# Toeplitz coefficients in pieces among projections, and zero rows written behind the input statistics

## The chip, the cores and the metric

One core of a Trainium2 chip runs one launch of the whole network. The metric is the device time of that launch in microseconds; the median of three runs of the kernel before is 5857.68 us. TensorE (PE) multiplies matrices into PSUM, VectorE (DVE) and ScalarE (ACT) read PSUM and SBUF, GpSimd (POOL) works on SBUF, and SyncE (SP) issues most DMA transfers; POOL issues some. Each engine takes its instructions in a fixed order.

## The reference

Four layers follow each other on x of shape (8, 56, 56, 192), each as `x = x + layer(groupnorm(x))`. Layers 0 and 1 are a gated Toeplitz block, layer 2 a depthwise convolution with an MLP, layer 3 window attention. The change concerns the first block (576 = D1 hidden channels):

```python
p, q, v = silu(x @ p_w.T + p_b), silu(x @ q_w.T + q_b), silu(x @ v_w.T + v_b)
gamma = (0.95 + 0.05 * clip(slope, 0, 1)) ** arange(1, n)
a1 = rpe_mlp(rpe_input, t1...) * decay     # 2n coefficients for each channel
a2 = rpe_mlp(rpe_input, t2...) * decay
qv = q * v
o1 = toeplitz(qv along the width, a1)
o2 = toeplitz(qv along the height, a2)
out = (p * (o1 + o2)) @ o_w.T + o_b
```

The coefficients `a1` and `a2` depend on weights alone: a small MLP of 32 units with three hidden layers, evaluated at 111 distances, times powers of a decay. The group norm in front of the block needs the mean and variance of each sample pair's whole input.

## The kernel before

Samples lie in four pairs j = 0 to 3, channels on partitions, tokens along the free axis (T = 3136). The first stage of `tno_layers` goes as follows.

`input_stats` loads the input of a pair in seven tiles `x` of 448 tokens (pool `tab`, seven buffers, line 213), VectorE takes their statistics (line 215), and `pair_gn_finish` turns them into scale and shift `gn` (lines 71 to 97).

`tno_qv` makes q*v for two pairs. Tiles `t6` of 256 tokens are loaded, normalized by ScalarE (line 243) and multiplied by the weights `wq` on TensorE in units of 128 tokens by up to 512 output columns (`unit`, line 260). Each tile of 128 tokens has two units of 512 columns and one of 128. VectorE moves a unit out of PSUM with the bias added (line 269, into one of three `t8` buffers), ScalarE takes SiLU (line 298), GpSimd multiplies q by v (line 301, into one of three `t4` buffers), and SyncE stores the product to `qv` in DRAM (line 304). The first four tiles of tokens are done as half units (lines 281 and 288, kept in buffers `z0` to `z11`), first for pair 0 and then for pair 1, since pair 1's statistics come later. All PSUM results rotate through four `bank2` tiles.

`decay_tables` makes the Toeplitz coefficients of one layer. VectorE makes powers of the decay into five `pw` tiles (lines 146 to 158). For each of the two directions it evaluates the MLP: line 175 the input layer, line 179 three matmuls with VectorE's ReLU (line 181) after each, line 185 five matmuls for the outputs. VectorE multiplies each output by the powers into a tile `a` (line 192, two buffers, cleared at the end by GpSimd, line 189), and SyncE writes it with a shift per row to the table in DRAM (line 202, 240 KB matrices are read from it later at line 389). The function is called once for each layer: 12 matmuls at line 179, 20 at line 185 and 72 table writes in both.

Two more writes fill what the Toeplitz stage reads beyond the data. A tile `none` of zeros is copied by a DMA of GpSimd's queue to the last eight rows of each image in both `qv` arrays (line 715, 4032 KB each), and four small ones to the last row of each table (line 719).

The order of this stage is not that of the source alone: the tile framework's scheduler orders it for each engine by dependences and its own estimates. From `in_order` on (the Toeplitz stage) TensorE, ScalarE, VectorE and GpSimd keep the order written. There `weave` runs the Toeplitz of one half beside the projections or outputs of another: it advances one generator as `lane` and calls the other, `steps`, for as much work as is due. A generator yields the time that its last piece is thought to take; `weave` spreads a total of `given` between the shares `lo` and `hi` of the lane.

The SP queue carries all loads, q*v stores and table writes in one order. In the kernel before, both zero writes stand at the head of GpSimd's queue, and each layer's 36 table writes stand in one block in SP's.

Of the kernel before, what the change touches and what calls it, by code (L numbers as in the profile page):

```python
# [12 lines left out]
F32 = mybir.dt.float32  # L13
# [16 lines left out]
TT = 448  # L30
NT = T // TT
D1 = 576
# [6 lines left out]
def view(ap, offset, dims):  # L39

    return bass.AP(ap.tensor, ap.offset + offset, [ap.ap[0], *dims])


class Net:
# [91 lines left out]
    def decay_tables(self, L, p, tables):  # L136

        nc, inp = self.nc, self.inp
        tv = p.tile([32, 111], F32, name="tv", bufs=1)
        nc.sync.dma_start(tv, inp["tvec"])  # L140
        pows = []
        for c in range(5):
            m = min(128, D1 - 128 * c)
            sl = p.tile([128, 1], F32, name="sl")
            nc.sync.dma_start(sl[:m], inp[f"{L}_slope"][128 * c : 128 * c + m, :])
            nc.vector.tensor_scalar(sl[:m], sl[:m], 0.0, 1.0, ALU.max, ALU.min)
            nc.vector.tensor_scalar(sl[:m], sl[:m], 1.0 - 0.95, 0.95, ALU.mult, ALU.add)
            pw = p.tile([128, 64], F32, name="pw", bufs=5)
            nc.gpsimd.memset(pw[:m, 0:1], 1.0)
            n = 1  # L150
            while n < 64:
                nc.vector.tensor_scalar(
                    pw[:m, n : 2 * n], pw[:m, 0:n], sl[:m], None, ALU.mult
                )
                n *= 2
                if n < 64:
                    sq = p.tile([128, 1], F32, name="sl")
                    nc.vector.tensor_mul(sq[:m], sl[:m], sl[:m])
                    sl = sq
            pows.append(pw)  # L160
        for d in range(2):
            t = f"{L}_t{d + 1}"
            w0 = p.tile([32, 2], F32, name="w0")
            nc.sync.dma_start(w0[:, 0:1], inp[f"{t}_w0"])
            nc.sync.dma_start(w0[:, 1:2], inp[f"{t}_b0"])
            ws = p.tile([32, 3, 32], F32, name="ws")
            nc.sync.dma_start(ws, inp[f"{t}_ws"])
            bs = p.tile([32, 3], F32, name="bs")
            nc.sync.dma_start(bs, inp[f"{t}_bs"])
            wo = p.tile([32, D1], F32, name="wo")  # L170
            nc.sync.dma_start(wo, inp[f"{t}_wo"])
            bo = p.tile([128, 5], F32, name="bo")
            nc.sync.dma_start(bo, inp[f"{t}_bo"])
            h = p.tile([32, 111], F32, name="h")
            nc.vector.tensor_scalar(h, tv, w0[:, 0:1], w0[:, 1:2], ALU.mult, ALU.add)
            nc.vector.tensor_scalar(h, h, 0.0, None, ALU.max)
            for i in range(3):
                hp = self.bank2()[:32, 0, :111]
                nc.tensor.matmul(hp, ws[:, i, :], h, start=True, stop=True)
                h = p.tile([32, 111], F32, name="h")  # L180
                nc.vector.tensor_scalar(h, hp, bs[:, i : i + 1], 0.0, ALU.add, ALU.max)
            for c in range(5):
                m = min(128, D1 - 128 * c)
                ap = self.bank2()[:, 0, :111]
                nc.tensor.matmul(
                    ap[:m], wo[:, 128 * c : 128 * c + m], h, start=True, stop=True
                )
                a = p.tile([128, 4 * self.TG + 56], F32, name="a")
                nc.gpsimd.memset(a[:m, 111:], 0.0)
                back = view(pows[c][:m], 55, [[-1, 55]])  # L190
                for lo, hi, dec in ((0, 55, back), (55, 111, pows[c][:m, 0:56])):
                    nc.vector.scalar_tensor_tensor(
                        view(a[:m], 110 - lo, [[-1, hi - lo]]),
                        ap[:m, lo:hi],
                        bo[:m, c : c + 1],
                        dec,
                        ALU.add,
                        ALU.mult,
                    )
                for n in range(m // 32):  # L200
                    to = tables[d][self.TG * (4 * c + n) : self.TG * (4 * c + n + 1)]
                    nc.sync.dma_start(
                        to.rearrange("g (c w) -> c g w", w=self.TW),
                        view(a[32 * n : 32 * n + 32], 0, [[4, self.TG], [1, self.TW]]),
                    )

    def input_stats(self, xs, gn, j, p):

# [457 lines left out]
    def tno_layers(self, x0, x1, x2, gn, last):  # L666


        tc, nc = self.tc, self.nc
        LS = ("L0", "L1")  # L670
        tables = [

            [
                self.dram.tile([D1 // 32 * self.TG + 1, 32 * self.TW], F32, name=f"{L}_tab{d}")
                for d in range(2)
            ]
            for L in LS
        ]
        qvs = {

            j0: self.dram.tile([D1 // 32, 64 * W, 128], F32, name=f"qv{j0}") for j0 in (0, 2)
        }
        o = [self.dram.tile([B // 2, 9, 128, T], F32, name=f"{L}_sum") for L in LS]
        x = (x0, x1, x2)
        with ExitStack() as ctx, ExitStack() as wqp:
            self.wqp = wqp.enter_context(tc.tile_pool(name="wqp", bufs=1, side="right"))
            self.tp = ctx.enter_context(tc.tile_pool(name="tp", bufs=3))
            Q = lambda i, j0, apart=None: self.tno_qv(LS[i], j0, x[i], gn[i], qvs[j0], apart)
            O = lambda i, j0, woven=True: self.tno_out(LS[i], j0, x[i], gn[i], o[i], x[i + 1], gn[i + 1], woven)
            TZ = lambda i, j0: self.tno_toeplitz(j0, tables[i], qvs[j0], o[i])  # L690
            QT, OT, TZT = 25 * 2.25 * 5.3, 28 * 10.7, 8 + 72 * 3.2

            with tc.tile_pool(name="tab", bufs=2) as tab:
                stats = [self.input_stats(x0, gn[0], j, tab) for j in range(4)]
                for more in stats[0]:
                    pass
                first = Q(0, 0, tab)
                next(first)

                for n in range(14):  # L700
                    next(first)
                    next(stats[1], None)
                for more in stats[1]:
                    pass
                for n in range(10):
                    next(first)
                self.decay_tables("L0", tab, tables[0])
                for st in stats[2:]:
                    for more in st:
                        next(first)  # L710
                none = tab.tile([112, 512], F32, name="none", bufs=1)
                nc.gpsimd.memset(none, 0.0)
                for qv in qvs.values():
                    to = qv[:, T:].rearrange("n (p k) e -> p n (k e)", p=112)
                    nc.gpsimd.dma_start(to, view(none, 0, [[0, D1 // 32], [1, 512]]))
                self.decay_tables("L1", tab, tables[1])
                for t in tables:
                    for d in range(2):
                        nc.gpsimd.dma_start(t[d][D1 // 32 * self.TG :, :512], none[:1])
                lanes = [[(first, QT - 104.0)], [(Q(0, 2), QT)], [(O(0, 0), OT), (Q(1, 0), QT)]]  # L720
                lanes += [[(O(0, 2), OT), (Q(1, 2), QT)], [(O(1, 0), OT)], [(O(1, 2, False), OT)]]
                self.weave(lanes[0], None, lanes[1][0][0])
            in_order = tc.manual_schedule(engines=ENGINES)
            with tc.tile_pool(name="tz", bufs=1) as self.tz, in_order:
                self.tms = []
                for i in range(2):
                    self.tms.append(self.tz.tile([128, 32 * self.TW], F32, name=f"tm{i}"))
                for n, tz in enumerate((TZ(0, 0), TZ(0, 2), TZ(1, 0), TZ(1, 2))):
                    self.weave(lanes[n + 1], tz, lanes[n + 2][0][0], TZT)
                    if n == 2:  # L730
                        wqp.close()
            self.weave(lanes[5], **last())
# [908 lines left out]
```

## Time and profile before

| what | us |
|---|---|
| median of 3 runs | 5857.68 (5851.6 to 5859.38) |
| profiled execution, its own time | 5859.99 |
| span of its trace | 5858.2 |
| mean granted TensorE clock | 0.954 |
| seventh x tile's statistics start | 41.49 |
| first projection matmul (L281) | 52.68 |
| first matmul of full units (L260) | 154.51 |
| first Toeplitz matmul (L402) | 507.65 |

Busy time over the span: PE 5356.5 us (91%), DVE 2365.6 us (40%), ACT 2269.0 us (39%), POOL 2206.4 us (38%). In the page's slices, a digit is the busy share of 146 us in tenths. A row of a window table gives start and end, length, busy time and count for each engine, then the granted TensorE clock, the mean busy share of the 16 DMA engines and their rate in GB/s. In a timeline row, the bracket holds the idle time before the instruction and what ended it. The count of TensorE rows is that of passes, two for each float32 matmul.

### The profile page before, as it was taken

The numbers are of one execution on the slowest core, as the hardware profiler recorded it, in microseconds if no ns is written. First come the engines' busy times: TensorE is split into PE (matmuls) and PEld (weight loads), VectorE is DVE, ScalarE is ACT, GpSimd is POOL, SyncE is SP. The second block draws the span as 40 slices with busy tenths as digits, with TensorE's granted clock in tenths as the row PEclk, the third lists the DMA queues.
The fourth block names the chain that finished last, engine by engine and source line by source line (L and its number), as shares of the span: only waits on it lengthen the run. The fifth ranks groups of instructions, "written<-read, shape, count | busy, mean of one in ns | idle before, by whom it ended". The sixth has DMA issues, their size and how long they took to land.

```text
span 5858.2 us, 144266 instructions
## 1 busy us (share of the span) xinstructions
PE 5356.5 (91%) x64672; PEld 3886.7 (66%) x64672; DVE 2365.6 (40%) x3770; ACT 2269.0 (39%) x2990; POOL 2206.4 (38%) x1527
## 2 busy tenths in 40 slices
PE   5799888899999999999888799989999999889887
PEld 2577666677777777777666578856665445667666
DVE  5444554233454233553343322331222322556655
ACT  2244454444454444554444322242323333333332
POOL 1244566466556564565666300000001001333332
PEclk8799999999999999999999899999999999999998
DMA  8547998898787887987999465644444222344442
GB/s 268 110 144 219 267 287 245 220 264 275 214 237 217 239 258 224 254 249 196 312 296 293 168 210 205 230 125 161 150 160 121 64 64 62 75 97 86 89 92 56
DMA packets 1029770, 1098.79 MB, mean 188 GB/s; under 512 B 232768, under 2 KB 966976, under 8 KB 1013728
## 3 DMA queue, kind: packets, MB, share of 16 engines
q1 hardware_dynamic: 993568, 888.57, 55.5%
q0 software_dynamic: 35584, 200.99, 8.9%
q8 instruction: 509, 8.34, 0.6%
q14 instruction: 109, 0.89, 0.0%
HBM read 725.48 MB, written 363.94 MB: 186 GB/s over the span
## 4 chain that ended last, share of the span: by engine, by line
PE 57%; POOL 6%; SPq 6%; DMA 5%; DVE 5%; issue 3%; ACT 2%; POOLq 0%; DVEq 0%; ACTq 0%
PE bank L260 9%; PE bank L950 6%; PE bank L811 5%; PE bank L527 4%; PE bank L1030 4%; PE bank L572 4%; PE bank L402 4%; SPq L389 3%; PE bank L1044 3%; POOL s L424 2%; PE bank L1224 2%; PE bank L536 2%; PE bank L575 2%; SPq L376 2%; PE bank L1171 2%
## 5 line engine op out<-in xcount | busy, mean ns | idle before, releaser
L260 PE MATMUL bank<-wq,t 128*128 128x256 f32 (+4 forms) x7680 | 1286.6, 375 | 66.8 <-DVE t L269 36.3
L260 PEld LDWEIGHTS bank<-wq,t 128*128 128x128 f32 (+2 forms) x7680 | 1006.5, 191 | 348.1 <-issue 110.5
L269 DVE TENSOR_TENSOR t<-bank,wq 128x1024 f32<-128x1024 f32 (+3 forms) x480 | 517.8, 1111 | 776.6 <-PE bank L260 575.1
L301 POOL TENSOR_TENSOR t<-t 128x1024 f32<-128x1024 f32 (+2 forms) x288 | 518.7, 1815 | 692.4 <-ACT t L298 371.5
L409 ACT COPY ot<-bank 128x896 f32<-128x896 f32 x576 | 493.2, 914 | 626.8 <-PE bank L402 351.3
L424 POOL TENSOR_TENSOR s<-s,ot 128x1568 f32<-128x1568 f32 x144 | 618.3, 4298 | 70.0 <-DVE ot L422 69.3
L402 PE MATMUL bank<-q,tm 56*32 56x224 f32 x18432 | 525.6, 365 | 81.6 <-DMA tm<-L_tab 26.8
L298 ACT ACTIVATE t<-t 128x2048 f32<-128x2048 f32 (+2 forms) x288 | 422.0, 1488 | 405.7 <-DVE t L269 396.1
L402 PEld LDWEIGHTS bank<-q,tm 56*32 56x32 f32 x18432 | 354.4, 109 | 221.6 <-issue 115.8
L553 POOL TENSOR_TENSOR t<-t,t 128x896 f32<-128x896 f32 x168 | 347.3, 2085 | 358.4 <-DMA t<-L_sum 163.9
L527 PE MATMUL bank<-t,wo 128*128 128x224 f32 x1792 | 398.0, 378 | 46.6 <-ACT t L506 22.1
L585 DVE SCALAR_TENSOR_TENSOR t<-bank,wo,t 128x448 f32<-128x448 f32 x112 | 76.4, 682 | 886.3 <-ACT t L581 474.7
L950 PE MATMUL bank<-z,w 128*128 128x448 f32 (+1 forms) x1344 | 413.7, 555 | 1.9 <-ACT h L959 1.7
L527 PEld LDWEIGHTS bank<-t,wo 128*128 128x128 f32 x1792 | 352.4, 203 | 83.8 <-issue 31.7
L546 ACT ACTIVATE t<-bank,wo 128x448 f32<-128x448 f32 x448 | 248.1, 635 | 407.2 <-PE bank L536 379.2
L572 PE MATMUL bank<-t,wo 128*128 128x224 f32 x1792 | 378.1, 365 | 0.0
L127 POOL DMA_DIRECT2D x<-x x64 | 36.6, 573 | 859.7 <-DVE x L981 829.6
L572 PEld LDWEIGHTS bank<-t,wo 128*128 128x128 f32 x1792 | 337.2, 194 | 33.8 <-issue 32.2
L811 PEld LDWEIGHTS bank<-xt,cm 113*112 113x112 f32 x3072 | 315.0, 180 | 43.7 <-issue 38.3
L420 DVE STREAM_TRANSPOSE s<-ot 128x1792 f32<-128x1792 f32 x144 | 292.5, 2033 | 124.3 <-DMA L_sum<-s 102.1
L811 PE MATMUL bank<-xt,cm 113*112 113x108 f32 (+2 forms) x3072 | 326.2, 266 | 6.4 <-issue 3.3
L950 PEld LDWEIGHTS bank<-z,w 128*128 128x128 f32 (+1 forms) x1344 | 182.2, 189 | 205.7 <-issue 197.4
(148 smaller groups left out, 6991.3 us busy)
## 6 DMA issues: line engine op xcount, KB each, us to landing
q<-qv SPq DMA_DIRECT2D x36, 3584.0 KB
q<-qv SPq DMA_DIRECT2D x72, 1568.0 KB
L_sum<-s POOLq DMA_DIRECT2D x288, 392.0 KB, 7.4
t<-L_sum SPq DMA_DIRECT2D x112, 1008.0 KB
qv<-t SPq DMA_DIRECT2D x192, 512.0 KB
cm<-in_L_cm SPq DMA_DIRECT2D x96, 896.0 KB
tm<-L_tab SPq DMA_DIRECT2D x288, 240.0 KB
x<-t POOLq DMA_DIRECT2D x112, 336.0 KB, 7.1
```

Source lines behind the costliest of these rows:

```text
L260: nc.tensor.matmul(pp[:m, b, 256 * j : 256 * j + k], x[rows, j, 2 if part else b, s : s + m], w[rows, part, c0 + c : c0 + c + k],  start=p ...
L269: nc.vector.tensor_add(z[:m, c : c + k, :], view(pp[:m], 0, [[1, k], [256, 4]]), view(bias[:m], c0 + c, [[1, k], [0, 4]]),)
L298: nc.scalar.activation(z[:m, :n, :], z[:m, :n, :], AF.Silu)
L301: nc.gpsimd.tensor_mul(prod[:m, :k], half[:, :, 0], half[:, :, 1])
L402: nc.tensor.matmul(pt[32 * j : 32 * j + 32, r, hf * 224 : (hf + 1) * 224], tm[rows, at : at + 32], q[rows, :, 4 * c : 4 * c + 4], start=Tr ...
L409: nc.scalar.copy(view(ot, 4 * (g % 4), [[16, 2], [32, 112], [1, 4]]), view(pt, 0, [[512, 2], [4, 112], [1, 4]]),)
L424: nc.gpsimd.tensor_add(to, to, view(of, 0, [[1, 28], [32, 56]]))
L527: mm(gs[c // 2][:, b, c % 2 * 256 : c % 2 * 256 + N], pw[:, 0, 128 * c : 128 * c + 128], xn[:, b], start=c % 2 == 0, stop=False,)
L553: gate.tensor_mul(to, to, pg)
L572: mm(P[:, b, :N], ow[:, c, 0:128], g[:, 4 * b + c], start=False, stop=c == 3 and b == 1)
L811: nc.tensor.matmul(pc[:, 128 * e + 4 * m0 : 128 * e + 4 * m1], cm[:113, e, k, :], xt[:, m0 - 1 + k : m1 - 1 + k, c + e, :], start=n == 0 a ...
L950: nc.tensor.matmul(phs[c][:, s, :TT], w0[rows, part, at : at + 128], z[rows, Z[2 if part else s], :], start=part == flip, stop=part != flip,)
```

## The change

`decay_tables` becomes a generator that yields after each tile of powers, each hidden layer and each output piece: 21 pieces a layer. Both layers' pieces are chained in `decay`. Fourteen are taken in turn with the statistics of pairs 2 and 3 and the half units, the other 28 by `weave` among the projections of the first half, spread over the first 75% of what is left of them. The small zero rows of the tables are written first, from a tile of one row. The zeros for `qv` no longer have a tile of their own: an `x` buffer is cleared after the last statistics' loads, so the clear waits until that buffer's statistics are taken, and the two big writes read from it.

```diff
@@ decay_tables
             pows.append(pw)
+            yield 1.0
         for d in range(2):
...
                 h = p.tile([32, 111], F32, name="h")
                 nc.vector.tensor_scalar(h, hp, bs[:, i : i + 1], 0.0, ALU.add, ALU.max)
+                yield 1.0
             for c in range(5):
...
                         view(a[32 * n : 32 * n + 32], 0, [[4, self.TG], [1, self.TW]]),
                     )
+                yield 1.0
@@ tno_layers
                 for n in range(10):
                     next(first)
-                self.decay_tables("L0", tab, tables[0])
+                none = tab.tile([1, 512], F32, name="none", bufs=1)
+                nc.gpsimd.memset(none, 0.0)
+                for t in tables:
+                    for d in range(2):
+                        nc.gpsimd.dma_start(t[d][D1 // 32 * self.TG :, :512], none)
+                decay = (dt for i in range(2) for dt in self.decay_tables(LS[i], tab, tables[i]))
                 for st in stats[2:]:
                     for more in st:
                         next(first)
-                none = tab.tile([112, 512], F32, name="none", bufs=1)
-                nc.gpsimd.memset(none, 0.0)
+                        next(decay)
+                rows = tab.tile([128, 3, TT], F32, name="x", bufs=7)[:112].rearrange("p k t -> p (k t)")
+                nc.gpsimd.memset(rows[:, :512], 0.0)
                 for qv in qvs.values():
                     to = qv[:, T:].rearrange("n (p k) e -> p n (k e)", p=112)
-                    nc.gpsimd.dma_start(to, view(none, 0, [[0, D1 // 32], [1, 512]]))
-                self.decay_tables("L1", tab, tables[1])
-                for t in tables:
-                    for d in range(2):
-                        nc.gpsimd.dma_start(t[d][D1 // 32 * self.TG :, :512], none[:1])
+                    nc.gpsimd.dma_start(to, view(rows, 0, [[0, D1 // 32], [1, 512]]))
                 lanes = [[(first, QT - 104.0)], [(Q(0, 2), QT)], [(O(0, 0), OT), (Q(1, 0), QT)]]
                 lanes += [[(O(0, 2), OT), (Q(1, 2), QT)], [(O(1, 0), OT)], [(O(1, 2, False), OT)]]
-                self.weave(lanes[0], None, lanes[1][0][0])
+                self.weave(lanes[0], decay, lanes[1][0][0], 28.0, 0.0, 0.75)
```

## The prediction

> **What bounds the kernel now.** I read the page's slices first, then busy time by stage, the DMA queues of the first 60 us, and TensorE's timeline and waits up to the first Toeplitz matmul.
>
> ```profile
> span 5858.2 us, 144266 instructions
> PE   5799888899999999999888799989999999889887
> PEclk8799999999999999999999899999999999999998
> ```
> TensorE is nearly full except in the first two slices of 146 us; that stretch is all that the diff touches.
>
> ```profile
> 0.00:41.50 41.50, 0.00 (x0) 0.00 (x0) 10.09 (x19) 0.00 (x0) 5.91 (x22) 1.00 0.97 361
> 52.70:119.20 66.50, 64.97 (x216) 27.56 (x216) 57.99 (x150) 24.17 (x31) 13.07 (x7) 0.95 0.68 222
> 119.20:154.50 35.30, 9.37 (x34) 5.37 (x33) 16.61 (x36) 9.25 (x13) 9.20 (x13) 0.56 0.88 180
> 154.50:245.80 91.30, 76.39 (x433) 60.68 (x433) 43.25 (x99) 31.31 (x30) 25.95 (x23) 0.89 0.47 121
> 245.80:269.00 23.20, 9.53 (x33) 5.38 (x32) 7.18 (x38) 0.26 (x1) 1.50 (x6) 0.50 0.73 125
> 269.00:288.50 19.50, 16.88 (x81) 12.66 (x81) 4.82 (x7) 3.82 (x3) 3.12 (x3) 0.79 0.41 68
> 288.50:507.70 219.20, 219.20 (x1361) 172.70 (x1362) 91.91 (x89) 95.64 (x98) 91.23 (x53) 1.00 0.52 141
> ```
> (Window, length, busy PE, PEld, DVE, ACT, POOL, granted clock, DMA share, GB/s.) Up to 41.5 us nothing runs but transfers, at their limit. Two stretches, 119.2 to 154.5 and 245.8 to 269.0, are the Toeplitz tables of the two layers: TensorE does 9.4 and 9.5 us of work in 58.5. From 288.5 the projections fill TensorE: 17 tiles of 128 tokens in 219.2 us, so 12.89 us a tile, 5.73 a unit of 512 columns. This is the rate to which the rest is held.
>
> ```profile
> q1 hardware_dynamic: 7778, 13.52, 63.1%
> q0 software_dynamic: 2176, 8.27, 36.3%
> x<-in_x SPq DMA_DIRECT2D x14, 672.0 KB
> qv<-none POOLq DMA_DIRECT2D x2, 4032.0 KB, 39.7
> ```
> First 60 us: the zeros (8.27 MB) are over a third of the traffic, at 363 GB/s in all, and land 39.7 us after issue: beside the seven x tiles, not after them.
>
> ```profile
> 142.32 0.73 PE L185 MATMUL bank<-h,wo 32*128 32x111 f32 x2 [5.58 <-DVE a L192]
> 145.45 0.73 PE L185 MATMUL bank<-h,wo 32*128 32x111 f32 x2 [2.39 <-DVE a L192]
> 149.17 0.73 PE L185 MATMUL bank<-h,wo 32*128 32x111 f32 x2 [2.99 <-DVE a L192]
> 154.51 4.58 PE L260 MATMUL bank<-wq,t 128*128 128x256 f32 x16 [1.33 <-issue]
> 160.41 3.06 PE L260 MATMUL bank<-wq,t 128*128 128x256 f32 x16 [1.33 <-DVE t L269]
> ```
> Each table piece waits for VectorE, which waits for a free `a`, that is for the table's transfers (28.6 us in "DVE a L192 <- DMA L_tab<-a"). Then the first projections run cold: 4.58 us for what later takes about 2.9.
>
> **What the Trainium skill says.** "DMA: Bandwidth & Descriptors", section "Issuing engines are not separate DMA queues": transfers of SyncE, ScalarE and GpSimd run on the same 16 engines and interleave. The trace agrees: an x tile's statistics start only every 5.6 to 7.6 us while the zeros run. "TensorE: Matmul & The Clock Gate", section "What's actually happening": an idle TensorE falls to half clock, and some 3.4 us of activity restores it. The granted clock of 0.50 in the second table stretch, and the 4.58 us above, agree. "SBUF — State Buffer", section "Who interferes with whom": tensor_scalar on VectorE can be blocked for the whole of a GpSimd instruction. The trace has L152 at 0.22 us in the median and 2.27 at most, close to GpSimd's 2.35 us product.
>
> **The change part by part**, for the profiled execution (5859.99 us, span 5858.2; the median of the runs is 5857.68, 2.3 less).
>
> *Zeros.* Behind the table coefficients' small zero rows, they now stand on GpSimd after the seventh product of q*v, from an x buffer whose statistics are done. Without their 8.27 MB the first sample's x lands 8.27 MB / 363 GB/s = 22.8 us earlier, and so do wq and the first t tiles. The fixed chain from the last x to the first projection (41.5 to 52.7) stays. **-22.8.** Written later, at about 95 us, they run beside the last x tiles (0.67 MB each), t tiles and stores of 0.5 MB. The projections use 141 GB/s of about 363, so there is room. Bounds: 0 with x landed before, as the order suggests (the last x is issued before the seventh product's store); 13 us if two x tiles and a t tile (2.1 MB) share half the rate and VectorE stops at the last statistics. I take **+2**. The two issues cost GpSimd 1.2 us each, in its idle time; nothing compute-side reads the zeros before the Toeplitz load.
>
> *Table of L0.* Its 16 matmul steps (6 of 0.57 us at L179, 10 of about 0.52 at L185) remain, 8.6 us, now one between two projection units. VectorE's arrears at the end of the half units also remain: TensorE stands 8.0 us at 119.6 until VectorE reaches `h`. One more x tile's statistics now lie ahead of that (3 x 0.61 + 0.73 us), so I keep 10. 35.3 - 8.6 - 10: **-16.7.**
>
> *Table of L1.* 23.2 - 8.6: **-14.6.**
>
> *Cold restarts.* 154.5 to 170.9 holds two units worth 11.5 us: 4.9 lost. 269.0 to 288.5 holds one tile, 12.9: 6.5 lost. Without the pauses, **-11.4.**
>
> *Norms of samples 3 and 4.* Two pauses of 8.4 and 11.8 us (191.1 to 199.5, 234.1 to 245.8). In the second the deviation waited 7.6 us for VectorE, busy with powers; in the new order its four steps follow at once. It goes to about 8: **-4.**
>
> *What the pieces add.* (1) GpSimd clears L1's five `pw`, which are the five buffers of L0. In the order of the built changed program each clear stands ahead of a product and waits for the last reader, L194 of the second L0 table. For the first two, that reader comes only after the projection whose output buffer (`t8`, three of them) that product must free; then product (2.35 us) and eviction (1.2) follow one another with TensorE waiting, past what the four PSUM tiles cover. About 2.5 us each, bounds 0 and 5: **+5.** (2) Each clear of `a` also stands among the products and waits for the transfers two pieces back. At one piece per 6 us they should be home (before, VectorE waited 1.5 to 5.8 us a piece with the pieces back to back); but where a product is ahead, VectorE waits up to 1 us. 18 such: bounds 0 and 18, **+3.** (3) On SyncE the 72 table writes stand mostly in fours among stores, where before 36 held the queue for 54 us at a time; the stores gain. The first q load stands behind two more stores, but the second q load is what gates: **+1**, bounds 0 and 5. Powers of L1 (30 tensor_scalars) were among running projections before too (219 to 240 us, six units in 34.7 us): nothing more.
>
> Sum: -22.8 - 16.7 - 14.6 - 11.4 - 4 = -69.5; +2 +5 +3 +1 = +11; **-58.5**. From the first Toeplitz matmul on, the order on TensorE, VectorE, ScalarE and GpSimd is as before, so the 5,350 us behind 507.7 shift as one piece. 5860.0 - 58.5 = 5801.5; at the median's level **5799**.
>
> **Rivals.**
> A, all of it hides: the four costs are nothing and the ten us of arrears shrink, since VectorE starts with x already there. Gain 69.5 + 10 = 80: 5778. For it: VectorE is busy for 92 of 219 us in steady projections. Against: clears in a strictly ordered GpSimd queue.
> B, the pieces stall one by one: twenty pieces at 2 to 2.5 us each (a tensor_scalar caught behind a product, a clear, a small transfer), instead of 8 us in all: 32 to 42 more. 5831 to 5841.
> C, slower: the same queue, but a whole unit. If every one of the twenty `a` pieces holds GpSimd until its transfer has come through SyncE behind a store that itself waits for GpSimd, each costs a unit of 5.73 us: 115 against 69.5, 5858 + 45 = 5903. It turns slower from 69.5/20 = 3.5 us a piece. For it: SyncE and GpSimd did wait on one another before (GpSimd 17.7 us on stores). Against: the transfers have two pieces' time, 11 us, and the waits for them were at most 5.8 (9.7 on GpSimd).
> D, nothing arrives at the end: the Toeplitz stage behind is DMA-bound (0.98 of the engines, 507.7 to 1000) and eats the start. Against: its bytes stay the same and no transfer of it was being done early, but for table loads of 1.9 MB (314 to 341 us). 5850 to 5858. That the zeros are not moved at all is excluded by the order.
>
> **How the numbers follow.** Chances: the forecast 0.60, A 0.17, B 0.14, C 0.05, D 0.04. The forecast's own ends: all four costs at nothing, 5788; at their upper ends (13 + 10 + 18 + 5 instead of 11), 35 more, 5834. A's and part of B's times are taken in: 5772 to 5830. A measurement of this kernel can tell about 0.2%, 11.7 us, from no change. Faster by more than that: the forecast, A, B: 0.92. Within: most of D, 0.03. Slower: 0.05.
>
> **What would show it.** First projection matmul at about 30 us in place of 52.7, no zeros in the first 60 us; no stretch of TensorE under half busy between 130 us and the Toeplitz start; that start at about 449 us in place of 507.7. "POOL pw L149 <- DVE a" with two waits that TensorE shares confirms (1); "DVE a <- DMA L_tab" near nothing confirms (2). "DVE st <- DMA x" late in the half units would show the zeros in the way. Wrong it would be if the projections between tables took over 7 us a unit, or if the Toeplitz stage took longer than before.

## The result, and the profile after

| | before | after |
|---|---|---|
| median of the runs, us | 5854.94 (5851.6 to 5859.38) | 5811.99 (5804.89 to 5817.99) |
| span of the profiled execution, us | 5858.2 | 5809.3 |
| first projection matmul, us | 52.7 | 27.8 |
| first matmul of full units, us | 154.5 | 96.2 |
| first Toeplitz matmul, us | 507.7 | 456.5 |

The change makes the kernel faster: ratio 0.9924, 95% interval 0.9911 to 0.9936 (four runs each; the medians differ by 43 us). The forecast was 5799, 13 us too low; the time lies in the range. In the file after, most lines stand 1 to 5 further down: L179, L185, L189 and L192 are L180, L187, L191 and L194; L243, L260, L269, L298, L301 and L304 are L246, L263, L272, L301, L304 and L307; L402 is L405. The clear of the `x` buffer is L721 and the zero writes are L724.

The page after, the same lines as those shown of before:

```profile
span 5809.3 us, 144273 instructions
...
PE   6998888999999999998898889999999999989987
...
PEclk9999999999999999999999899999999999999998
```
The half-empty start (57 in the first two digits of before) has become 69, and the first two clock digits, 87, have become 99. Behind that, the work is the same. The windows from the first Toeplitz matmul to the end, of before and then of after:

```profile
507.70:5858.00 5350.30, 4954.72 (x62498) 3597.08 (x62496) 2130.13 (x3324) 2102.29 (x2814) 2056.43 (x1404) 0.96 0.65 189
```

```profile
456.50:5809.00 5352.50, 4957.35 (x62498) 3598.57 (x62496) 2129.70 (x3324) 2102.95 (x2814) 2057.45 (x1404) 0.96 0.65 189
```
The same counts on every engine, 5350.3 and 5352.5 us long: everything behind the Toeplitz start came forward as one piece. The start of the Toeplitz stage therefore measures the change, 51.2 us in these two profiles, and does so better than one run's total, since this last stretch differs between the profiles of the experiments below by up to 14 us (5342 to 5356) with the same work in it.

Up to that start the kernel after shows what was gained and what was given back. TensorE's timeline:

```profile
27.76 22.93 PE L284 MATMUL bank<-wq,t 128*128 128x512 f32 x64 [2.74 <-ACT t L246]
...
103.43 25.03 PE L263 MATMUL bank<-wq,t 128*128 128x256 f32 x136 [5.21 <-DVE z L291]
142.67 3.23 PE L263 MATMUL bank<-wq,t 128*128 128x128 f32 x16 [14.21 <-DVE t L272]
...
174.61 0.47 PE L187 MATMUL bank<-h,wo 32*128 32x111 f32 x2
175.01 5.65 PE L263 MATMUL bank<-wq,t 128*128 128x256 f32 x32
```
The projections begin 25 us earlier. The table pieces (L187) cost 0.47 us each between two units that run at full rate (5.65), where before TensorE waited 2.4 to 5.6 us in front of those that the prediction shows. But there is a stop of 14.21 us at 128.5, where the prediction has nothing: the arrears that it kept at 10 us are the 5.21 in front of 103.43.

The waits of the engines between 95 and 145 us (engine, what it waited for; total, times, longest):

```profile
POOL t L304 <- DMA qv<-t: 27.6, 2, 27.2
DVE t L272 <- POOL t L304: 22.4, 2, 22.0
ACT t L246 <- DMA t<-in_x: 21.4, 1, 21.4
...
PE bank L263 <- DVE t L272: 14.2, 1, 14.2
```
Read from below: TensorE has no free PSUM tile until VectorE empties one; VectorE has no free `t8` buffer until GpSimd has multiplied; GpSimd has no free `t4` buffer until a store of q*v has landed. At the end of the chain stands one store, for which GpSimd waits 27.2 us. Beside it ScalarE waits 21.4 us for a tile of input:

```profile
130.51 3.06 ACT L246 ACTIVATE t<-t,gn 128x256 f32<-128x256 f32 x6 [21.36 <-DMA t<-in_x]
133.48 4.21 ACT L301 ACTIVATE t<-t 128x2048 f32<-128x2048 f32 x3
```
In ScalarE's order the SiLU of the first full units (L301) stands behind the normalization of that tile (L246), and GpSimd needs this SiLU for its product at 139.02, whose end lets VectorE go on at 141.39. So there are two late transfers side by side. Had the store alone come in time, the stop would have ended some 4 us earlier and not 14: an estimate from the end of the first SiLU (133.48 + 1.91) and one product of 2.35 us. What the queues moved between 97 and 131 us, and what GpSimd did:

```profile
q0 software_dynamic: 2044, 8.25, 72.7%
q1 hardware_dynamic: 3801, 3.06, 27.6%
```

```profile
97.03 1.18 POOL L724 DMA_DIRECT2D qv<-x  x1 [0.30 <-POOL x L721]
98.21 3.03 POOL L304 TENSOR_TENSOR t<-z 128x1024 f32<-128x1024 f32 x2
105.39 2.37 POOL L304 TENSOR_TENSOR t<-z 128x1024 f32<-128x1024 f32 x1 [4.16 <-ACT z L301]
107.69 1.15 POOL L724 DMA_DIRECT2D qv<-x  x1
136.03 3.03 POOL L304 TENSOR_TENSOR t<-z 128x1024 f32<-128x1024 f32 x2 [27.18 <-DMA qv<-t]
```
The zeros, 8.25 of 11.34 MB in those 34 us, fill the DMA engines (busy share 1.01, 334 GB/s with the rest) as they did at the start of the kernel before (0.97, 361 GB/s), only that now computation waits for the transfers beside them. GpSimd issues the two writes 10.7 us apart, with three products between them, and stands still from 108.8 to 136.0.

### The profile page after: what moved, and what is told of

It is laid out like the page before. It is cut to its first block, busy times and chain, and to the rows that moved or that the text cites. A ratio compares the mean times of both kernels' runs of the same rounds, so it can differ in the third digit from the quotient of the medians.

```text
span 5809.3 us, 144273 instructions
## 1 busy us (share of the span) xinstructions
PE 5361.1 (92%) x64672; PEld 3889.9 (67%) x64672; DVE 2365.9 (41%) x3770; ACT 2269.1 (39%) x2990; POOL 2207.7 (38%) x1528
## 4 chain that ended last, share of the span: by engine, by line
PE 59%; SPq 9%; DMA 9%; POOL 9%; DVE 7%; issue 4%; ACT 2%; POOLq 0%; DVEq 0%; ACTq 0%
PE bank L263 12%; PE bank L955 7%; PE bank L816 5%; PE bank L1035 4%; SPq L392 4%; PE bank L530 4%; POOL s L427 4%; PE bank L405 4%; PE bank L575 3%; DMA qv<-t 3%; SPq L379 3%; PE bank L1049 3%; DMA t<-L_sum 3%; PE bank L539 2%; PE bank L578 2%
## 5 line engine op out<-in xcount | busy, mean ns | idle before, releaser
L263 PE MATMUL bank<-wq,t 128*128 128x256 f32 (+4 forms) x7680 | 1293.7, 376 | 81.4 <-DVE t L272 41.6
L263 PEld LDWEIGHTS bank<-wq,t 128*128 128x128 f32 (+2 forms) x7680 | 1009.5, 191 | 359.5 <-issue 103.5
L272 DVE TENSOR_TENSOR t<-bank,wq 128x1024 f32<-128x1024 f32 (+3 forms) x480 | 517.7, 1112 | 774.0 <-PE bank L263 554.7
L304 POOL TENSOR_TENSOR t<-t 128x1024 f32<-128x1024 f32 (+2 forms) x288 | 519.5, 1818 | 650.0 <-ACT t L301 326.7
L405 PE MATMUL bank<-q,tm 56*32 56x224 f32 x18432 | 523.0, 362 | 83.6 <-DMA tm<-L_tab 27.5
L301 ACT ACTIVATE t<-t 128x2048 f32<-128x2048 f32 (+2 forms) x288 | 421.9, 1488 | 398.2 <-DVE t L272 394.8
L405 PEld LDWEIGHTS bank<-q,tm 56*32 56x32 f32 x18432 | 352.6, 108 | 221.2 <-issue 117.5
```

What stands on the lines that cost most here:

```text
L263: nc.tensor.matmul(pp[:m, b, 256 * j : 256 * j + k], x[rows, j, 2 if part else b, s : s + m], w[rows, part, c0 + c : c0 + c + k],  start=p ...
L272: nc.vector.tensor_add(z[:m, c : c + k, :], view(pp[:m], 0, [[1, k], [256, 4]]), view(bias[:m], c0 + c, [[1, k], [0, 4]]),)
L301: nc.scalar.activation(z[:m, :n, :], z[:m, :n, :], AF.Silu)
L304: nc.gpsimd.tensor_mul(prod[:m, :k], half[:, :, 0], half[:, :, 1])
L405: nc.tensor.matmul(pt[32 * j : 32 * j + 32, r, hf * 224 : (hf + 1) * 224], tm[rows, at : at + 32], q[rows, :, 4 * c : 4 * c + 4], start=Tr ...
```

## The experiments

The theory on record is that the zeros cost about 2 us in their new place and the table pieces about 9 by their waits. The rival, formed on the profile after: the zeros cost some 20 us there, and the pieces almost nothing. (The first expectations call this rival theory 1; their theory 2 puts the stop down to the order of the table pieces.) Each experiment is a small edit of the kernel after. "T" is the time from the first half-unit projection to the first Toeplitz matmul: 428.7 in the kernel after.

### Each part alone

`zeros_only` makes each layer's table in one go, as before, and leaves the zeros in their new place:

```diff
-                decay = (dt for i in range(2) for dt in self.decay_tables(LS[i], tab, tables[i]))
+                for more in self.decay_tables("L0", tab, tables[0]):
+                    pass
...
-                        next(decay)
...
+                for more in self.decay_tables("L1", tab, tables[1]):
+                    pass
...
-                self.weave(lanes[0], decay, lanes[1][0][0], 28.0, 0.0, 0.75)
+                self.weave(lanes[0], None, lanes[1][0][0])
```

> The zeros moved, the tables made whole as before. Theory 1 (the moved zeros hold SyncE's stores of q*v for some 30 us: GpSimd then has no free t4, VectorE no free t8, TensorE stops): first projection at 27.8 us as in the change; the zeros then run during the whole first table block, where TensorE stands anyway, and lengthen it somewhat, so the Toeplitz starts at 485 to 500 us instead of 507.7, and the time is 5836 to 5850. Theory 2 (the table pieces in GpSimd's and SyncE's order make the stop, the zeros do not): full gain of 25 us at the start, Toeplitz at 483, time 5830.

`tables_only` keeps the pieces and puts the zeros back to the head of GpSimd's queue:

```diff
-                rows = tab.tile([128, 3, TT], F32, name="x", bufs=7)[:112].rearrange("p k t -> p (k t)")
-                nc.gpsimd.memset(rows[:, :512], 0.0)
+                none = tab.tile([112, 512], F32, name="none", bufs=1)
+                nc.gpsimd.memset(none, 0.0)
...
-                    nc.gpsimd.dma_start(to, view(rows, 0, [[0, D1 // 32], [1, 512]]))
+                    nc.gpsimd.dma_start(to, view(none, 0, [[0, D1 // 32], [1, 512]]))
```

> The tables in pieces, the zeros written at the head as before. Theory 1: first projection at 52.7 us, no stop of TensorE over 6 us in the 50 us after the half units, Toeplitz at 455 to 462 us, so about the time of the whole change, 5805 to 5816: what the zeros give at the start they take back later. Theory 2: the stops of 5 and 14 us stay, 25 us later than in the change, Toeplitz at 481, time 5836.

| | first projection | first Toeplitz matmul | T | median us, ratio to before |
|---|---|---|---|---|
| before | 52.7 | 507.7 | 455.0 | |
| zeros_only | 28.4 | 493.1 | 464.7 | 5849.06, 0.9983 (0.9973 to 0.9993) |
| tables_only | 52.9 | 461.0 | 408.1 | 5816.37, 0.9932 (0.9914 to 0.9951) |
| after | 27.8 | 456.5 | 428.7 | 5811.99, 0.9924 (0.9911 to 0.9936) |

The tables in pieces bring 46.7 us at the Toeplitz start (507.7 to 461.0). The zeros' move brings 25 us at the first projection and keeps 4.5 of them at the Toeplitz start (461.0 to 456.5), too little for the run times to tell (the intervals of tables_only and after overlap). In the other order the shares differ: the zeros' move alone brings 14.6 us (507.7 to 493.1), and the pieces added to it 36.6. The two get in each other's way by 10.1 us. In either order the pieces are the larger part and much of the zeros' 25 us is lost again, as the rival has it. Where the 20.6 us between after and tables_only go is seen when both kernels are cut at the same points of TensorE's work. The windows of after, then of tables_only: to the first full unit, to the first output piece of the first table, and so on.

```profile
27.80:96.20 68.40, 64.86 (x216) 28.03 (x216) 60.82 (x146) 23.09 (x31) 13.15 (x8) 0.95 0.73 244
96.20:166.90 70.70, 50.34 (x257) 39.45 (x255) 26.56 (x48) 25.06 (x28) 24.28 (x16) 0.78 0.75 239
166.90:220.00 53.10, 51.73 (x301) 41.54 (x301) 21.34 (x43) 18.72 (x16) 12.62 (x12) 0.90 0.43 102
220.00:240.00 20.00, 18.15 (x107) 13.97 (x106) 11.57 (x21) 8.36 (x8) 10.22 (x11) 1.00 0.65 166
240.00:456.50 216.50, 213.16 (x1280) 163.07 (x1276) 101.93 (x162) 88.72 (x92) 86.30 (x62) 0.98 0.63 156
```

```profile
52.90:121.30 68.40, 64.83 (x217) 27.98 (x217) 60.73 (x146) 23.15 (x31) 13.17 (x7) 0.95 0.70 229
121.30:171.40 50.10, 44.30 (x257) 34.72 (x255) 25.81 (x48) 25.12 (x28) 21.58 (x12) 0.93 0.57 172
171.40:224.70 53.30, 51.93 (x302) 41.71 (x302) 21.52 (x43) 18.71 (x16) 12.80 (x12) 0.90 0.43 102
224.70:244.70 20.00, 18.15 (x107) 13.99 (x107) 11.38 (x21) 8.36 (x8) 10.21 (x11) 1.00 0.67 170
244.70:461.00 216.30, 212.99 (x1278) 162.88 (x1274) 101.91 (x162) 88.72 (x92) 85.89 (x62) 0.98 0.64 156
```
Four of the five stretches agree to 0.2 us. The second holds the same 257 passes of TensorE and takes 70.7 in place of 50.1: the whole 20.6. Of these, 14.6 are idle time (20.4 against 5.8 without work) and 6.0 are busy time (50.34 against 44.30): the same matmuls at a lower granted clock (0.78 against 0.93 in the mean of the stretch, its idle time included). Behind the stop the clock is 0.50 from 142.7 to 149.7. The steps there, of after and then of tables_only:

```profile
145.83 0.57 PE L180 MATMUL bank<-h,ws 32*32 32x111 f32 x2
146.33 7.38 PE L263 MATMUL bank<-wq,t 128*128 128x256 f32 x32
```

```profile
153.88 0.37 PE L180 MATMUL bank<-h,ws 32*32 32x111 f32 x2
154.18 5.65 PE L263 MATMUL bank<-wq,t 128*128 128x256 f32 x32
```
With the 16 passes ahead of them (3.23 us at 142.67, 1.80 at full rate) they take 3.4 us more than in tables_only: the clock adds a quarter of the stop again. The other 2.6 us of slower matmuls are not shown to come from the stop: 1.0 lies ahead of it, behind the arrears, and 1.6 behind the pause for the next norm. The unit there takes 8.03 us (7.31 in tables_only), but 7.92 in half_zeros and 8.69 in gated_zeros below, which have no such stop.

In zeros_only the scheduler put the writes later, at 179.4 and 194.4 us, behind the first table; beside it was expected. So it is in part luck that start and time came out as expected. TensorE stops for 10.93 us at 194.9. There VectorE waits for another transfer, the small load of a decay slope (line 145; 10.89 us). The victim differs, the stop goes with the zeros.

### The dose

`half_zeros` leaves one of the two writes at the head of GpSimd's queue, so that 4.13 MB come behind the half units; `double_zeros` writes both arrays twice there.

```diff
+                to = qvs[2][:, T:].rearrange("n (p k) e -> p n (k e)", p=112)
+                nc.gpsimd.dma_start(to, view(none, 0, [[0, D1 // 32], [1, 512]]))
...
-                for qv in qvs.values():
+                for qv in (qvs[0],):
```

> The change with the zeros of the second half of the samples (4.13 MB) written at the head as before, those of the first half at the change's place. Theory 1: start 11 to 12 us later than in the change (first projection at 39 to 40), stop after the half units reduced to 5 to 12 us from 19; Toeplitz at 450 to 458 us. If the stop came from the order of SyncE's transfers alone it stays at 19 and the Toeplitz comes at 468.

```diff
-                for qv in qvs.values():
+                for qv in (qvs[0], qvs[2], qvs[0], qvs[2]):
```

> The change with each of the two large zero writes issued twice (same values, 16.5 MB in place of 8.26 MB at the same place). Theory 1: the stop grows by the time of 8.26 MB, 20 to 26 us, Toeplitz at about 480 us, time 5832 to 5838. Theory 2: as the change, Toeplitz at 457, time 5812.

| zeros behind the half units | kernel | T | more than tables_only | of it TensorE idle |
|---|---|---|---|---|
| 0 | tables_only | 408.1 | | |
| 4.13 MB | half_zeros | 413.8 | 5.7 | 3.3 |
| 8.26 MB | after | 428.7 | 20.6 | 14.6 |
| 16.5 MB | double_zeros | 443.4 | 35.3 | 27.1 |

More bytes, more time, but not in proportion. The first half costs 5.7 us, the second 14.9. In half_zeros GpSimd still waits 15.3 us for one store, but TensorE stops for only 2.8 us in all, in three places: the buffers between them (three `t4`, three `t8`, four PSUM) take up the rest. The doubled zeros grew by 14.7 where 20 to 26 were expected; GpSimd, held up by the stop, issued the second pair only at 142.8 and 149.6, so that it is a second burst and not a longer one. One execution each (5811.92 and 5818.6 us; Toeplitz starts 453.9, as expected, and 471.2, where about 480 was); the half one starts its projections at 40.1, as half of the zeros lies ahead of x again. What of T is not idle time is slower matmuls, and the stretches at half clock fall on other units in other runs (the unit that takes 7.50 us at 204.11 in after takes 5.65 in wo_pool below), so that differences of T of 2 or 3 us settle nothing.

### The same bytes in smaller doses

`gated_zeros` cuts the zeros into four writes of 2.06 MB. They wait for the scale `gn` of a pair of samples, by one VectorE instruction that writes into the tile of zeros: one write for pair 1, one for pair 2, two for pair 3. So there are doses of 2.06, 2.06 and 4.13 MB, some way apart in the stage:

```diff
+                def zeros(j, *parts):
+                    rows = tab.tile([112, 512], F32, name="rows", bufs=2)
+                    nc.gpsimd.memset(rows, 0.0)
+                    nc.vector.tensor_scalar(rows[:, :1], gn[0][:112, j, 0, 0:1], 0.0, None, ALU.mult)
+                    for j0, n in parts:
+                        to = qvs[j0][:, T:].rearrange("n (p k) e -> p n (k e)", p=112)
+                        nc.gpsimd.dma_start(to[:, n : n + 9], view(rows, 0, [[0, 9], [1, 512]]))
...
+                zeros(1, (0, 0))
...
+                    zeros(j, *([(0, 9)] if j == 2 else [(2, 0), (2, 9)]))
```

> The change with the zeros in four writes of 2 MB from tiles of their own, each held back by one VectorE write that reads a norm's result: the first after the norm of pair 1 (about 60 us, where few transfers run), the second after that of pair 2, two after that of pair 3; no t4 is taken. Theory 1 (8.26 MB at one place behind the half units make the stop): no stop over 6 us after the half units, Toeplitz at 430 to 438 us, time 5786 to 5796. Rival (the zeros cost their transfer time wherever they stand before the Toeplitz): Toeplitz at 450 to 462 us, as in the change and in the spread version.

Measured: T 411.6, Toeplitz start 440.0 (2 us outside what was expected), median 5793.98, ratio 0.9887 (0.9868 to 0.9906). The best kernel of the study: its median is 18 us below that of the kernel after, and 61 below that of the runs of before beside it. GpSimd issued the writes at 58.8, 146.2, 190.0 and 193.3. TensorE's timeline has no stop of the kind:

```profile
106.12 26.88 PE L263 MATMUL bank<-wq,t 128*128 128x256 f32 x152 [4.63 <-DVE z L291]
...
141.54 1.77 PE L78 MATMUL bank<-gn_dev,pmat 128*128 128x2 f32 x12 [0.93 <-DVE gn_dev L92]
```
The arrears of 4.63 us are followed by 152 passes in a row, and the zeros' cost against tables_only has gone from 20.6 to 3.5 us, of which 2.7 lie in the half units, beside the first write.

`late_burst` asks whether it is the place or the dose: all four writes at the last of these gates, where gated_zeros has two.

```diff
+                    if j == 3:
+                        zeros(j, (0, 0), (0, 9), (2, 0), (2, 9))
```

> gated_zeros with all four writes after the norm of pair 3 (about 200 us), 8.26 MB in one burst among steady projections. If a burst of this size is what makes the stop, wherever it stands: stops of 8 us or more of TensorE at 205 to 235 us, first projection to Toeplitz 420 to 430 us (411.6 in gated_zeros, 428.7 in the change). If it is the place behind the half units, where loads stand ahead of the stores in SyncE's queue: no stop, 408 to 414.

```profile
210.04 3.78 PE L263 MATMUL bank<-wq,t 128*128 128x256 f32 x8 [4.58 <-DVE t L272]
...
231.07 6.63 PE L263 MATMUL bank<-wq,t 128*128 128x256 f32 x24 [17.25 <-DVE t L272]
```
Issued between 186.5 and 192.6, the burst stops TensorE for 4.58 and 17.25 us at 205 to 231; T is 430.1, 22.0 more than without zeros. (One execution, 5802.41.) VectorE waits 19.8 us there for a clear of `a` that stands in GpSimd's queue behind a product waiting for a store to land, and ScalarE 30.0 us for a tile of input. In gated_zeros, with 4.13 MB at the same gate, the longest stop between 188 and 235 us is this one:

```profile
208.76 3.06 PE L263 MATMUL bank<-wq,t 128*128 128x256 f32 x16 [0.81 <-DVE t L272]
```
So it is the dose, as the first reading has it (T 0.1 above its range): no stop above 0.81 us for 4.13 MB, 17 us and more for 8.26 at one place. With zeros_only, that is a burst in three places, with a stop each time and a different piece of work late.

`spread_zeros` cuts finer still, into twelve pieces that borrow a `t4` buffer each, one after every second table piece. Its other edit, not shown here, spreads tables and zeros over 85% of what is left of the projections, where the kernel after has 75% for the tables:

```diff
+                        for n in range(0, D1 // 32, 3):
+                            rows = self.tp.tile([128, 4, DC * 4], F32, name="t4")[:112]
+                            nc.gpsimd.memset(rows[:, :2], 0.0)
+                            nc.gpsimd.dma_start(to[:, n : n + 3], view(rows, 0, [[0, 3], [1, 512]]))
+                            yield 1.0
```

> The change with the zeros written in twelve pieces of 3 planes (688 KB) from t4 buffers, one after every second table piece among the projections. Theory 1: no stop after the half units, Toeplitz at 430 to 438 us, time 5786 to 5795. Theory 2: as the change or slower by the twelve clears on GpSimd (12 x 0.6 us), 5812 to 5820.

Toeplitz start 462.9, median 5815.83, ratio 0.9932 (0.9913 to 0.9952): no better than the kernel after, and T is 434.4. (That is the time that theory 2 gave; the waits show another reason than its twelve clears.) The big stop behind the half units is gone (no stop of TensorE behind them is over 4.8 us until the Toeplitz start), but the waits between 125 and 465 us show a new price:

```profile
POOL t L304 <- DMA qv<-t: 39.7, 8, 7.6
...
DVE t L272 <- POOL a L191: 32.0, 4, 9.4
...
PE bank L405 <- issue: 10.9, 1, 10.9
```
Each piece takes one of the three buffers that the products need, so GpSimd waits eight times for a store to land, and VectorE four times for GpSimd, whose clears of `a` stand behind such waits. TensorE also stands 10.9 us in front of the Toeplitz matmuls, for which the profile shows no releaser; that part stays open. So small doses do away with the big stop, and these waits point to the borrowed buffer as the new price; no run has the same pieces with buffers of their own.

### Who is late: the engines or the queue?

While the zeros run, SyncE takes about 2 us for each transfer that it issues. The timeline of its queue in the kernel after:

```profile
105.49 1.93 SPq L165 DMA_DIRECT2D w<-in_L_t_w  x1
...
112.23 2.11 SPq L492 DMA_DIRECT2D wo<-in_L_pw  x1
...
118.84 2.02 SPq L492 DMA_DIRECT2D wo<-in_L_ob  x1
120.95 27.62 SPq L307 DMA_DIRECT2D qv<-t  x9
```
and the same transfers in tables_only, without zeros beside them:

```profile
138.59 0.42 SPq L165 DMA_DIRECT2D w<-in_L_t_w  x1
139.06 0.41 SPq L166 DMA_DIRECT2D w<-in_L_t_b  x1
139.52 0.42 SPq L492 DMA_DIRECT2D wo<-in_L_pw  x1
```
The store that GpSimd waits for is issued at 120.95, behind four loads of output weights that nobody needs yet. `wo_pool` issues these four from GpSimd:

```diff
-            nc.sync.dma_start(to, inp[f"{L}_{name}"])
+            nc.gpsimd.dma_start(to, inp[f"{L}_{name}"])
```

> The change with the output weights' four loads (1.06 MB) issued by GpSimd instead of SyncE, so that they no longer stand ahead of the stores of q*v while the zeros run. If only the bytes in flight count: the stop is 3 us shorter, Toeplitz at 453 to 456. If each transfer ahead of the stores in SyncE's queue costs its issue interval, 2.1 us then: the stores come 8.7 us earlier and the stop is 7 to 10 us shorter, Toeplitz at 447 to 450.

The store comes 8 us earlier, at 112.88, and the Toeplitz start is 448.9, 7.6 before that of after. But the stop itself shrank little: from 14.21 to 11.79 us with a new one of 1.82 ahead of it, and GpSimd's wait from 27.2 to 25.7. So the issue order is not most of the stop: the store that GpSimd waits for was issued 8 us earlier, and the wait was 1.5 us shorter. ScalarE's wait did not shrink (22.4 us), so that, by the estimate above, an earlier store could have gained little in any case. That the filled DMA engines hold both transfers back is the likely reason, but no run separates it. The other 7 us are nearly all the same units at a higher granted clock: 3.6 us between the first L180 behind the stop and the fourth (45.5 instead of 49.1), and 3.3 further on. As it is one execution, whether the edit has a part in that stays open.

### The clears of `pw`

The prediction's dearest wait, (1), should fall away with ten `pw` buffers in place of five, alone and together with the gated zeros (where the small zero rows of the tables also come from a tile of 32 columns in place of 512):

```diff
-            pw = p.tile([128, 64], F32, name="pw", bufs=5)
+            pw = p.tile([128, 64], F32, name="pw", bufs=10)
```

> The change with ten pw tiles. By the prediction's price the Toeplitz comes 3 to 6 us earlier than in the change, 451 to 454; if the clears' waits are hidden, within 2 us of 456.5. The stop of 14 us stays.

> gated_zeros with ten pw tiles in place of five, so that GpSimd's clears of L1's powers wait for no reader of L0's. If those waits (38 us on GpSimd in the change) cost TensorE what the prediction gave them, 5 us: Toeplitz 3 to 6 us earlier than gated_zeros. If products have slack enough: within 2 us of it.

Toeplitz starts 460.4 instead of 456.5, and 446.6 instead of 440.0; the second with a median of 5803.84, ratio 0.991 (0.9892 to 0.9928), against 0.9887 without it. Both starts lie outside of either reading of what was expected. The scheduler had put the work into another order: in pw10 the long stop is 14.49 us at 120.3, in gated_pw10 there are stops of 3.22 and 6.36 us between 120 and 143, which gated_zeros does not have. So the two kernels do not price the clears by themselves; they show that nothing was gained in this way.

## Why the prediction came out as it did

*Zeros, taken away at the start: -22.8.* Right: the first projection came 24.9 us earlier in after, 24.3 in zeros_only.

*Zeros, in the new place: "I take +2".* This is the step that failed. It measured 20.6, and its upper bound of 13 was too low as well (its own terms, 2.1 MB at half of 363 GB/s, give nearer 12). The reasoning was that the projections use 141 of some 363 GB/s, "so there is room". That rate is of the later projections; behind the half units, where the zeros went, tables_only moves 172 GB/s without them. But a mean rate is no room in any case when a burst of 8.26 MB fills every engine for 34 us (busy share 1.01 from 97 to 131): what counts is how long one store or load is delayed and how long the buffers carry, and three `t4` buffers did not carry 27 us. The bound looked for trouble at the statistics ("VectorE stops at the last statistics") and for x tiles arriving late; those were spared, and the store of q*v and the load of `t` were late instead. The chain had been on the table, in the kernel before: GpSimd waited on stores there too (the 17.7 us that the prediction names), but the prediction counted that for rival C alone. The sign that it named for the zeros in the way, a wait of VectorE for x tiles, did not show; but another of its signs failed, "no stretch of TensorE under half busy between 130 us and the Toeplitz start": the stop, from 128.5 to 142.7, is one. Nor did the bound have the cold clock behind a stop. The Trainium skill's sentence on it ("TensorE: Matmul & The Clock Gate", section "What's actually happening") was cited only for the pauses that vanish. The trace agrees here too: 3.4 us of slower matmuls behind the stop, at a granted clock of 0.50.

*Tables of L0 and L1, cold restarts, norms: -16.7 - 14.6 - 11.4 - 4, and the pieces' costs +5 +3 +1.* Together -37.7 was forecast, and tables_only measured -46.7. That this equals the gains alone is chance: the arrears behind the half units, kept at 10 us, were 4.9 in tables_only (4.31 + 0.56), which is 5 of the 9 us. The other 4 belong to the pieces' costs or to the gains; the single terms are not separated.

*What the pieces add: (1) +5, (2) +3, (3) +1.* Each is smaller where it can be seen. (1) is where the prediction put it. GpSimd waited 38.2 us for VectorE in front of the `pw` clears, once for 21.90:

```profile
218.44 0.10 POOL L149 MEMSET pw<- 128x1 f32 x1 [21.90 <-DVE a L194]
```
But TensorE lost only 1.2 and 0.6 us there (at 222.6 and 227.3), since the buffers between them took the rest; 1.9 us instead of 5. (2) is nearly absent: GpSimd waited 10.3 us for the table transfers (49.8 before), at most 2.3, and VectorE no longer has a wait for them of any size (28.6 us before). For (3) nothing shows.

*The shift as one piece.* Right: 5350.3 and 5352.5 us. Put together at the Toeplitz start: 449.2 was forecast, the zeros' net is 16.3 worse (-4.5 in place of -20.8) and the tables are 9 better (arrears and costs together), which makes 456.5, as measured. The total came out near because these two errors oppose each other: that is luck, and the range held it.

*The rivals.* A (all hides) fails for the zeros; for the tables the 46.7 lies midway between the forecast's 37.7 and A's 56.7. B expected a stop at each piece; there is one stop, and it is not at a piece. C failed on the waits for transfers, 2.3 us at most where 3.5 would decide. D failed: the Toeplitz start came 51.2 us earlier and the stretch behind it kept its length.

## What to carry to other kernels

In this kernel a large transfer that nobody waits for was not free beside computation that lives on small ones. Compare the time for which it fills the DMA engines with the time that the buffers of the tightest loop can bridge, not its bytes with the mean rate. If it is longer, cut it into pieces that each fit under the buffers, put them apart by something that really happens at different times, and do not take their source from the buffers of that loop. Here 4.13 MB at one place cost little and 8.26 MB some 20 us. Work that is independent of the main stream and leaves TensorE idle is best given out one small step at a time between units of the main stream: here that was worth 46.7 us alone, and 36.6 on top of the zeros' move. Two changes in one stage should be measured apart and together: these two brought 14.6 and 46.7 us alone, but 51.2 together.

## What the runs showed of the hardware

A burst of writes from GpSimd's queue also slows the issuing of SyncE's. A transfer of 0.1 KB took 0.4 us to issue without it (138.59 in tables_only) and 1.9 beside it (105.49 in after): ten transfers, most of them small, held the queue from 99.6 to 121 us. And TensorE paid for the stop beyond its length: 14.21 us without work were followed by 7 us at a granted clock of 0.50, and the first steps took 3.4 us more than the same steps in tables_only.
